# Values' inner products: one matmul of 256 moving columns, written to two places of a PSUM bank, instead of two of 128

## The chip, the cores and the metric

The kernel runs on one core of one Trainium2 chip. The metric is the device time of one execution in microseconds (us). The engines are called PE (TensorE, matmuls), PEld (the weight loads of TensorE, which overlap the matmuls), DVE (VectorE), ACT (ScalarE), POOL (GpSimd) and SP (SyncE, which issues the DMAs). All data are fp32. In the profile every fp32 matmul of the code shows as two MATMUL records, each with its own LDWEIGHTS: the code's 392 matmuls of the gates give 784 records at line 366.

## The reference, cut to what matters

The input x (1024 tokens of 512 features, two batches of 512 tokens) is layer-normalised to xn. Attention makes values and gates from it for 32 heads of 128 dimensions:

```
qkv  = silu(hidden_states @ qkv_w.T)         # q, k, v of every head
gate = sigmoid(hidden_states @ gate_w.T)
...                                          # decaying linear attention over blocks, RMS norm
return gate * normed @ out_w.T
```

A feed-forward part with low-rank experts is added. This case is about `v`, a third of `qkv`: xn times the values' weights, 1024 x 512 times 512 x 4096.

## The kernel before

There are two large stages. The first, the front stage (to about 432 us in the profile), normalises x and computes all values and all gates, which it stores to DRAM. The second computes queries and keys, the attention and the output product. Only the front stage holds the change.

**Sets, rounds, products.** The large products are done by Strassen's scheme in its seven-product form, at two levels. The front stage has eight sets (`n` = 0 to 7); a set is eight heads (two groups of four, `u` = 0 and 1), even sets are values and odd sets are gates. A set has seven outer products, called rounds (`q` = 1 to 7), 56 in all in the list `rounds`; a round has seven inner products (`i` = 1 to 7). An inner product fills one PSUM bank of 128 partitions x 512 fp32, for both groups.

**Which operand moves.** For gates (line 366) the weights `a[:, u]` are stationary and 256 tokens `x_` move: two matmuls, one for each `u`, each with 256 moving columns. For values (line 362) the tokens are stationary, in two pieces of 128 (`j`), and the weights of one group, 128 columns, move: four matmuls of 128 moving columns. The bank is laid out as (u, j, d), so the pieces `j` = 0 of both groups are not neighbours.

**Order.** A round is one turn of a loop over `SLOTS = ((0, 1), (0, 5), (0, 2), (1, 7), (0, 6), (0, 3), (1, 4))`: a pair is (rounds back, inner product). So products 7 and 4 of a round are done within the next one, and where a set of values meets a set of gates, lines 362 and 366 alternate. After each product, `after` says what follows: after product 1, ACT copies the bank `pa` to a new bank (line 427), and product 2, two slots later, adds onto `pa`, so that its first weight load waits for that copy. After product 6 ACT copies again (line 434). The other results are added by DVE (lines 401, 405, 413, 420) or copied by ACT (403, 422); finished ones get Silu or Tanh on ACT (379, 381) and are stored by a DMA on SP (383). The banks are three of tag `fr` and four named `sd` (`seeded`).

**Operands.** `encode` (on POOL, two rounds ahead) makes the weights' sums of a round: four small ones `e` of 128x256 (lines 191 to 194), and for some rounds one or two large ones `s` of 128x1024 (line 177). Products 3, 5, 6 and 7 read `e` (product 3 the last part), products 1, 2 and 4 read the set's weights `raw` or a large sum `s`. `load_set` loads a set's weights from where round `q` = 2 of the set before begins. The order on every engine is that of the code; semaphores come from the tile framework.

Of the kernel before, what the change touches and what calls it, by code (L numbers as in the profile page):

```python
# [40 lines left out]
P = 128  # L41
# [18 lines left out]
def attn_moe_kernel(ctx: ExitStack, tc: tile.TileContext, x, qk_w, v_w, gate_w, out_w, norm_w,  # L60
                    decay, base_w, base_b, router_a_w, lora_b, out):
    nc = tc.nc
# [135 lines left out]
    for n in range(NSET):  # L198
        start = {0: [(0, 1), (1, 1), (0, 6)], 1: [(1, 6), (0, 4)]}.get(n, [(n, 1), (n - 1, 4), (n, 6)])
# [154 lines left out]
    def inner_product(o, r, i, first):  # L354
        n, q = rounds[r]
        a = operand[n, q][i]
        x_ = {1: xo[q][:, 0, :HB], 2: xo[q][:, 1, :HB], 3: xo[q][:, 1, HB:], 4: xt[q - 1][:, 3],
              5: xt[q - 1][:, 0], 6: xt[q - 1][:, 1], 7: xt[q - 1][:, 2]}[i]
        for u in range(2):
            if n % 2 == 0:  # L360
                for j in range(2):
                    nc.tensor.matmul(o[:, (2 * u + j) * P : (2 * u + j + 1) * P], x_[:, j * P : (j + 1) * P],  # L362
                                     a[:, u], start=first and u == 0 and j == 0, stop=True,
                                     skip_group_check=True)
            else:
                nc.tensor.matmul(o[:, u * HB : (u + 1) * HB], a[:, u], x_, start=first and u == 0, stop=True,  # L366
                                 skip_group_check=True)
# [76 lines left out]
    for k in range(7 * len(rounds) + 7):  # L444
        r0, m = divmod(k, 7)
        if m == 0:
            if r0 + 2 < len(rounds):
                encode(*rounds[r0 + 2])
            if r0 < len(rounds):
                n, q = rounds[r0]  # L450
                state_of[r0] = {}
                for _, to in ADDED[q]:
                    if isinstance(to, str):
                        outer_sums[n, to] = aw2.tile([P, 4, 512], F32, tag="sum", name="sum", bufs=4)
                if q == 2 and 0 < n < NSET - 1:
                    load_set(n + 1)
                if (n, q) == (NSET - 1, 2):
                    load_pair(0)
                    for i in range(2):
                        load_unit(i)  # L460
        back, i = SLOTS[m]
        r = r0 - back
        if not 0 <= r < len(rounds):
            continue
        st = state_of[r]
        if i in (1, 5):
            st["pa" if i == 1 else "pc"] = bank("fr")
        inner_product(st[{1: "pa", 2: "pa", 5: "pc", 3: "pc", 6: "pb", 7: "pd", 4: "pd"}[i]], r, i, i in (1, 5))
        after(r, i)
# [182 lines left out]
    for i in range(H * B + 2):  # L652
        p, part = divmod(i, 4)
# [18 lines left out]
        for stage in range(3):  # L672
            j = i - stage
# [141 lines left out]
```

## Time and profile before

| | |
|---|---|
| median of three runs | 1240.96 us (1240.21 to 1243.94) |
| the profiled execution's own time | 1241.71 us |
| its span (first to last instruction) | 1239.9 us |
| PE busy | 1207.4 us, 97% of the span |
| DVE, POOL, ACT busy | 629.1, 592.8, 366.1 us |
| granted PE clock, mean | 0.993 |
| PE busy from 120 to 400 us | 276.7 of 280 us |

A row of the profile's list of groups reads: line, engine, operation, output<-input by the program's tile names, shapes, count, then busy time and mean duration of one, then the engine's idle time before such instructions and what ended it. Durations of neighbouring matmuls overlap, since a matmul's end lies after the next one's start; the pace of PE is therefore read from the starts of consecutive records, in the timeline. There a row gives the start, the length of the merged group, the engine, line, operation, tiles, shape and count.

### The profile page before, as it was taken

The numbers are of one execution on the slowest core, as the hardware profiler recorded it, in microseconds if no ns is written. First come the engines' busy times: TensorE is split into PE (matmuls) and PEld (weight loads), VectorE is DVE, ScalarE is ACT, GpSimd is POOL, SyncE is SP. The second block draws the span as 40 slices with busy tenths as digits, with TensorE's granted clock in tenths as the row PEclk, the third lists the DMA queues.
The fourth block names the chain that finished last, engine by engine and source line by source line (L and its number), as shares of the span: only waits on it lengthen the run. The fifth ranks groups of instructions, "written<-read, shape, count | busy, mean of one in ns | idle before, by whom it ended". The sixth has DMA issues, their size and how long they took to land.

```text
span 1239.9 us, 17100 instructions
## 1 busy us (share of the span) xinstructions
PE 1207.4 (97%) x6328; PEld 914.3 (74%) x6328; DVE 629.1 (51%) x1104; ACT 366.1 (30%) x648; POOL 592.8 (48%) x662
## 2 busy tenths in 40 slices
PE   6789999999999999999999999999999999999998
PEld 4369889899899745666666666666666669888887
DVE  5757666766766624444444434444444444455333
ACT  2124444444444422223222222222232332320000
POOL 3926568758756241434433433433333343655552
PEclk9989999999999999999999999999999999999999
DMA  8012543452442353343443443343334333843221
GB/s 315 0 68 75 173 151 121 153 170 96 161 161 103 123 166 91 119 135 112 145 140 103 125 134 102 117 125 118 116 114 128 120 97 108 309 150 122 93 92 52
DMA packets 102706, 158.17 MB, mean 128 GB/s; under 512 B 8800, under 2 KB 68192, under 8 KB 101344
## 3 DMA queue, kind: packets, MB, share of 16 engines
q1 hardware_dynamic: 102624, 157.09, 38.2%
q8 instruction: 50, 0.82, 0.3%
q14 instruction: 32, 0.26, 0.1%
HBM read 102.53 MB, written 54.53 MB: 127 GB/s over the span
## 4 chain that ended last, share of the span: by engine, by line
PE 93%; DVE 5%; issue 1%; ACT 1%; DMA 0%; SPq 0%; DVEq 0%; ACTq 0%
PE ps_ch L488 31%; PE ps_ch L645 9%; PE ps_at L80 8%; PE ps_sc L80 8%; PE ps_fr L362 7%; PE ps_fr L366 7%; PE sd L362 5%; PE sd L366 5%; PE ps_sc L645 4%; PE ps_at L645 2%; PE sd L80 2%; PE ps_sc L550 2%; DVE z L405 1%; DVE sum L405 1%; PE ps_ra L80 1%
## 5 line engine op out<-in xcount | busy, mean ns | idle before, releaser
L488 PE MATMUL ps_ch<-xsum,ws 128*128 128x512 f32 x384 | 180.0, 593 | 0.0
L562 POOL TENSOR_TENSOR qd<-q,mask 128x384 f32<-128x384 f32 x64 | 64.2, 1003 | 219.9 <-PE ps_at L80 214.8
L488 PE MATMUL ps_ch<-xnT,w 128*128 128x512 f32 x256 | 122.2, 600 | 0.8 <-DVE z L405 0.8
L488 PEld LDWEIGHTS ps_ch<-xsum,ws 128*128 128x128 f32 x384 | 68.5, 191 | 63.2 <-issue 63.2
L80 PEld LDWEIGHTS ps_at<-scores,v 128*128 128x128 f32 x512 | 77.4, 192 | 28.0 <-issue 27.7
L126 POOL TENSOR_TENSOR ws<-w 128x256 f32<-128x256 f32 x32 | 23.4, 730 | 154.3 <-DMA w<-in_qk_w 154.3
L503 DVE TENSOR_TENSOR c<-ps_ch,u 128x512 f32<-128x512 f32 x96 | 66.4, 691 | 58.4 <-PE ps_ch L488 58.4
L588 DVE SCALAR_TENSOR_TENSOR gT<-gate,ps_at 128x512 f32<-128x512 f32 x64 | 44.0, 687 | 97.5 <-ACT sq L585 94.5
L645 PE MATMUL ps_ch<-wsum,gsum 128*128 128x256 f32 x384 | 89.1, 379 | 0.0
L80 PE MATMUL ps_at<-scores,v 128*128 128x128 f32 x512 | 88.4, 275 | 0.0
L585 ACT ACTIVATE sq<-ps_at 128x512 f32<-128x512 f32 x62 | 37.0, 597 | 155.2 <-PE ps_at L80 155.1
L586 POOL TENSOR_TENSOR ssq<-ssq,sq 128x512 f32<-128x512 f32 x62 | 79.2, 1278 | 6.5 <-ACT sq L585 6.5
L645 PEld LDWEIGHTS ps_ch<-wsum,gsum 128*128 128x128 f32 x384 | 72.3, 190 | 9.5
L80 PE MATMUL ps_at<-qd,state 128*128 128x128 f32 x384 | 74.2, 275 | 0.0
L80 PEld LDWEIGHTS ps_sc<-v,kd 128*128 128x128 f32 x384 | 52.8, 191 | 28.4 <-issue 28.2
L633 POOL TENSOR_TENSOR wsum<-wo 128x256 f32<-128x256 f32 x32 | 25.3, 790 | 93.0 <-PE ps_ch L645 37.4
L488 PEld LDWEIGHTS ps_ch<-xnT,w 128*128 128x128 f32 x256 | 44.4, 192 | 34.2 <-issue 33.1
L503 DVE TENSOR_TENSOR u<-ps_ch,p 128x512 f32<-128x512 f32 x32 | 22.1, 692 | 91.4 <-PE ps_ch L488 85.5
L80 PE MATMUL ps_sc<-q,k 128*128 128x128 f32 x512 | 67.6, 275 | 0.0
L552 ACT ACTIVATE kd<-ps_sc,mask 128x384 f32<-128x384 f32 x64 | 37.2, 580 | 89.8 <-PE ps_sc L550 89.8
L626 DVE TENSOR_TENSOR gsum<-gated 128x256 f32<-128x256 f32 x32 | 15.1, 470 | 95.2 <-PE ps_sc L645 66.7
L80 PEld LDWEIGHTS ps_sc<-q,k 128*128 128x128 f32 x512 | 62.2, 192 | 0.0
(224 smaller groups left out, 2633.6 us busy)
## 6 DMA issues: line engine op xcount, KB each, us to landing
w<-in_qk_w SPq DMA_DIRECT2D x32, 512.0 KB, 4.1
v_kept<-z SPq DMA_DIRECT2D x64, 256.0 KB, 2.4
gate_kept<-z SPq DMA_DIRECT2D x64, 256.0 KB, 2.4
v<-v_kept SPq DMA_DIRECT2D x64, 256.0 KB, 2.6
gate<-gate_kept SPq DMA_DIRECT2D x64, 256.0 KB, 3.2
g_kept<-gT SPq DMA_DIRECT2D x64, 256.0 KB, 2.5
gated<-g_kept SPq DMA_DIRECT2D x32, 512.0 KB, 3.7
raw<-in_v_w SPq DMA_DIRECT2D x8, 1024.0 KB, 6.6
```

The costliest lines, as they stand in the source:

```text
L80: nc.tensor.matmul(o, lhsT, rhs, start=start, stop=stop)
L362: nc.tensor.matmul(o[:, (2 * u + j) * P : (2 * u + j + 1) * P], x_[:, j * P : (j + 1) * P], a[:, u], start=first and u == 0 and j == 0, st ...
L366: nc.tensor.matmul(o[:, u * HB : (u + 1) * HB], a[:, u], x_, start=first and u == 0, stop=True, skip_group_check=True)
L488: nc.tensor.matmul(o, a[:, c, :], b[:, c, :], start=first and c == 0, stop=c == 1, skip_group_check=True)
L503: nc.vector.tensor_tensor(o, p, t, ALU.add)
L552: nc.scalar.activation(kd.rearrange("p j d -> p (j d)"), pk[:, : (TB - 1) * P], AF.Copy, scale=mask[:, 0, P - 1 : P])
L562: nc.gpsimd.tensor_tensor(qd, q[:, P:].rearrange("p (j n) -> p j n", j=TB - 1), mask[:, 1, :].unsqueeze(1).to_broadcast([P, TB - 1, P]), A ...
L585: nc.scalar.activation(sq, pa, AF.Square)
L586: nc.gpsimd.tensor_tensor(ssq[b], ssq[b], sq, ALU.add)
L588: nc.vector.scalar_tensor_tensor(gT, gate.pop((head, b)), 1.0, pa, ALU.add, ALU.mult)
L633: nc.gpsimd.tensor_tensor(t[:, 0], b12, b11, ALU.subtract)
L645: nc.tensor.matmul(sums[n][:, i * HO : (i + 1) * HO], l[:, i * P : (i + 1) * P], r, start=p == 0 and i == 0, stop=p == NP - 1, skip_group_ ...
```

## The change

For values, the inner loop over `j` is gone. For each piece `u` of 128 tokens one matmul is issued; its moving operand is `a` whole, 128 columns of the first group and 128 of the second, and its output is two runs of 128 columns, 256 columns apart in the bank. (`u` in the new lines counts the pieces of tokens, and `g` the groups.) The values written and their places are the same.

```
         for u in range(2):
             if n % 2 == 0:
-                for j in range(2):
-                    nc.tensor.matmul(o[:, (2 * u + j) * P : (2 * u + j + 1) * P], x_[:, j * P : (j + 1) * P],
-                                     a[:, u], start=first and u == 0 and j == 0, stop=True,
-                                     skip_group_check=True)
+
+                nc.tensor.matmul(o.rearrange("p (g j d) -> p j g d", g=2, j=2)[:, u], x_[:, u * P : (u + 1) * P],
+                                 a, start=first and u == 0, stop=True, skip_group_check=True)
             else:
                 nc.tensor.matmul(o[:, u * HB : (u + 1) * HB], a[:, u], x_, start=first and u == 0, stop=True,
                                  skip_group_check=True)
```

An inner product of the values thus has 2 matmuls (4 records) in place of 4 (8 records). There are 4 even sets x 7 rounds x 7 products = 196 of them. The moving operand of products 3, 5, 6 and 7 is one run of 256 elements; of products 1, 2 and 4 it is two runs of 128, 512 elements apart in a sum `s` and 2048 apart in `raw`.

## The prediction

> **What bounds the kernel now.** I read the page's busy times first, then the chain that ended last, then, for the front stage alone, the timeline of PE and the waits. The busy times and the chain:
>
> ```profile
> PE 1207.4 (97%) x6328; PEld 914.3 (74%) x6328; DVE 629.1 (51%) x1104; ACT 366.1 (30%) x648; POOL 592.8 (48%) x662
> ...
> PE 93%; DVE 5%; issue 1%; ACT 1%; DMA 0%; SPq 0%; DVEq 0%; ACTq 0%
> PE ps_ch L488 31%; PE ps_ch L645 9%; PE ps_at L80 8%; PE ps_sc L80 8%; PE ps_fr L362 7%; PE ps_fr L366 7%; PE sd L362 5%; PE sd L366 5%; PE ps_sc L645 4%; PE ps_at L645 2%; PE sd L80 2%; PE ps_sc L550 2%; DVE z L405 1%; DVE sum L405 1%; PE ps_ra L80 1%
> ```
>
> PE is the bound and line 362 is 12% of the chain (7% and 5%), so time taken from it is on the path. How much a record costs is its distance to the next start, not its duration of 275 ns. The timeline of PE shows one undisturbed round of values (q = 7 of set 6), and one of gates (q = 7 of set 7):
>
> ```profile
> 367.10 1.06 PE L362 MATMUL ps_fr<-s,xsum 128*128 128x128 f32 x8
> 367.99 1.06 PE L362 MATMUL ps_fr<-e,xt 128*128 128x128 f32 x8
> 368.88 1.09 PE L362 MATMUL ps_fr<-s,xsum 128*128 128x128 f32 x8
> 369.81 1.95 PE L362 MATMUL sd<-e,xt 128*128 128x128 f32 x16
> 371.60 1.06 PE L362 MATMUL ps_fr<-e,xsum 128*128 128x128 f32 x8
> 372.49 1.06 PE L362 MATMUL sd<-s,xt 128*128 128x128 f32 x8
> 373.38 0.39 PE L362 MATMUL ps_fr<-s,xnT 128*128 128x128 f32 x2
> ```
>
> ```profile
> 410.74 1.03 PE L366 MATMUL ps_fr<-xsum,s 128*128 128x256 f32 x4
> 411.60 1.03 PE L366 MATMUL ps_fr<-xt,e 128*128 128x256 f32 x4
> 412.47 1.09 PE L366 MATMUL ps_fr<-xsum,s 128*128 128x256 f32 x4
> 413.39 1.89 PE L366 MATMUL sd<-xt,e 128*128 128x256 f32 x8
> 415.12 1.03 PE L366 MATMUL ps_fr<-xsum,e 128*128 128x256 f32 x4
> 415.98 1.03 PE L366 MATMUL sd<-xt,s 128*128 128x256 f32 x4
> 416.85 0.38 PE L366 MATMUL ps_fr<-xnT,s 128*128 128x256 f32 x1
> ```
>
> The reader should see that eight records of 128 columns take 0.89 us (367.10 to 367.99) and four of 256 take 0.86 (410.74 to 411.60). From the records to the nanosecond: 893 and 863 ns, that is 111.6 and 215.8 ns each. The third product of both rounds takes longer, 0.93 us: it is product 2, which waits for the copy of line 427. Whole rounds: 373.38 - 367.10 = 6.28 us against 416.85 - 410.74 = 6.11. The gates do the same amount of arithmetic in the shape that the values are to get.
>
> The waits tell of the copy:
>
> ```profile
> PEld ps_fr L366 <- ACT sd L427: 7.7, 27, 0.8
> ...
> PEld ps_fr L362 <- ACT sd L427: 2.3, 2, 2.0
> ```
>
> In nearly every gates' round the weight load of product 2 comes late; in values' rounds it is late too, but by less (0.04 us at 368.81, under what the list shows).
>
> **What the Trainium skill says.** "TensorE: Matmul & The Clock Gate", in "Wait — 56ns, not 53.3ns?", gives a fixed 2.5 ns per matmul on top of columns / 2.4 GHz. The trace agrees if an fp32 record is two cycles a column: 256 x 2 / 2.4 + 2.5 = 215.8 ns (215.8 measured) and 512: 429.2 (429 at line 488). For 128 it gives 109.2, which the transposes of line 550 have (109); line 362 has 111.6, 2.4 more. "Back-to-back issue gap" on that page says that weight load and matmul together set the spacing; the weight loads' shortest distance here is about 108 ns (412.425 to 412.533), so at 128 columns they are nearly the bound, and at 256 they are covered twice over. "PSUM — Partial Sum Buffer", "Specifications (TRN2)", says that any non-contiguous access slows matmuls significantly; "Advanced Engine Details and Errata", "PSUM Cachelines", narrows that to every two consecutive elements being contiguous. No matmul in this trace has more than one run in its moving operand, and the code has none before with two runs in its output, so neither can be checked yet. "SBUF — State Buffer", "SBUF: two separate sides", says that a DVE instruction with two SBUF inputs and a POOL one lock each other out; the trace agrees (below).
>
> **The change part by part.**
>
> 1. Records removed and lengthened: 196 products x (8 x 111.6 - 4 x 215.8 = 893 - 863 = 30 ns) = 5.9 us less on PE. This takes 215.8 ns for a record of two runs from line 366's one run; its bounds are in the rivals. The 784 weight loads that go (192 ns each) lie beside matmuls; their only cost on the path is the 2.4 ns per record counted here.
> 2. Given back at product 2, in each of the 28 values' rounds. The copy starts when product 1 is out and takes 0.57 us, and product 5, which covers it, becomes 30 ns shorter. In the rounds shown, products 5 and 2 take 894 + 927 ns with values and 864 + 927 with gates: the wait grows from 34 to 64 ns, 28 x 30 = 0.8 us. All later products queue behind that weight load; DVE and ACT get product 2 no later than in a gates' round.
> 3. More in rounds q = 5 and q = 6, where an ACT activation stands ahead of the copy. q = 5: a values' round lasts 367.10 - 360.78 = 6.32 us, a gates' 410.74 - 404.51 = 6.23, so that 0.09 is gained there and not 0.17: 4 x 0.08 = 0.3 us. q = 6: products 5 and 2 take 962 + 995 ns with values and 992 + 967 with gates, 30 ns more given back in three rounds, 0.1 us.
> 4. Semaphores, DMAs, POOL's, DVE's and ACT's instructions: the same number in the same order. The cover of POOL's sums shrinks with the rounds, by 0.17 us each. POOL waited 40.9 + 37.5 us for PE between 100 and 430 us, so it is ahead; without that lead, as around 150 to 165 us, where it is busy without a break, up to three values' rounds would pass their 0.5 us on as a wait.
> 5. What is late next: DVE where POOL locks it out. Where sets meet, a sum of two SBUF tiles meets a large sum on POOL:
>
> ```profile
> 155.88 2.80 POOL L177 TENSOR_TENSOR s<-raw 128x1024 f32<-128x1024 f32 x1
> ...
> 156.39 2.83 DVE L405 TENSOR_TENSOR z<-c,sum 128x512 f32<-128x512 f32 x1
> ...
> 159.80 0.58 ACT L427 COPY sd<-ps_fr 128x512 f32<-128x512 f32 x1
> ...
> 160.43 0.82 PE L362 MATMUL ps_fr<-raw,xnT 128*128 128x128 f32 x5 [1.82 <-ACT sd L427]
> ```
>
> The DVE sum takes 2.83 us for 0.68, the next activation waits for DVE, the copy stands behind it, and PE stands 2 us. Adding up how far products exceed the usual time at the six such crossings from 100 to 345 us gives about 0.9, 2.4, 0.4, 0.1, 0.6 and 1.4 us, 5.8 in all. Whether the two meet depends on tenths of a microsecond; the change shifts PE and DVE by that much against POOL, which follows the weights' DMAs there. I take no change on average. With some 0.8 us of spread per crossing, six of them spread by about 2 us to either side.
>
> Sum: 5.9 - 0.8 - 0.3 - 0.1 = 4.7 us, and 0.2 I take off for point 4: 4.5 us. The profiled execution took 1241.7 us (span 1239.9); it would take 1237.2. The median of the runs lies 0.75 below the profiled one: **1236.5 us**. The second stage is fed by PE alone at its start and moves forward whole: PE is busy for all of 500 to 1000 us.
>
> **The rivals.** A difference of 0.3%, 3.7 us, is about what a measurement of this kernel can tell from no change.
>
> *Gain eaten by the crossings, or by a record that is not as cheap as line 366's.* If collisions cost 3 us more than now, 1.5 us remain: about 1239.5. Much the same comes out if a two-run record costs 5 ns more than a one-run record (784 x 5 = 3.9 of the 5.9 us; most of point 2 then goes too): 1239. For it: one meeting cost 2 us in the trace, and point 4. Against it: crossings of both kinds are met now, and they may as well get better.
>
> *Slower, by the two runs.* If PE stops between the runs of an output, each of the 784 records pays. The point from which it decides is 5.9 us / 784 = 7.5 ns for equal time (what points 2 and 3 give back is then not taken either), and 7.5 + 3.7 / 784 = 12.2 ns for slower by 0.3%. As a price I take the 25 ns below which, by the TensorE page ("Wait — 56ns, not 53.3ns?"), no two matmuls start apart, as an estimate of a restart: 784 x 25 = 19.6 us, less 5.9: 1254.7. The sentence in the PSUM page speaks for it. Against it, the runs are 512 bytes long and even, so the narrower rule is met, as it is in the moving operand. The unknown is bounded below by the one-run record (no gain is in sight beyond: its 215.8 ns are the streaming time plus 2.5), and above by half speed, 784 x 216 = 169 us, which I hold for nearly excluded.
>
> *The change does nothing.* If a run costs what a matmul of its own did (111.6 ns), the time stays at 1241.
>
> **How the numbers follow.** The forecast (4.5 us give or take the crossings' 2) has 0.84: of it, about two thirds lie beyond 3.7 us. The eaten or void gain has 0.08, the slower rival 0.08. Hence faster 0.57, same 0.34 (0.27 from the forecast's lower part, 0.07 of the eaten gain), slower 0.09. The range reaches from a gain of 7.5 us to the eaten gain's far side: 1233.5 to 1241.5; left out are most of the slower rival and the tails.
>
> **What would show it right or wrong.** Right: in the timeline, the values' products as four records, 0.86 us from start to start, undisturbed rounds of 6.11 us, product 2 at 0.93 us with the weight load's wait for the copy now listed for values as for gates. Products 1 and 2, which read two runs, should pace like 5 and 6, which read one; if only 1 and 2 are slower, it is the read; if all are, it is the write. Wrong: a pace above 220 ns; the six crossings adding up to 8 us or more; or a stop on POOL's `e`. A start of the second stage (432 us now) not 4 to 5 us earlier would say that the front stage gave the gain back.

## The result, and the profile after

The changed kernel takes 1238.41 us (median of 22 runs, 1235.25 to 1241.49) against 1240.74 us before (22 runs, 1237.82 to 1244.18): the ratio is 0.9981 with a 95% interval from 0.9972 to 0.9990. A second series gave 0.9988 (0.9979 to 0.9997; 22 runs against 27). The change is a gain of 2.4 us by the first ratio and 1.5 us by the second, where 4.5 were forecast. The time lies in the range, which is 8 us wide; the gain is about half of the forecast, or less.

The profiled execution took 1238.33 us. The page's busy times and its chain, as for the kernel before (the lines after the change have numbers one lower):

```profile
PE 1200.8 (97%) x5544; PEld 882.8 (71%) x5544; DVE 628.3 (51%) x1104; ACT 366.4 (30%) x648; POOL 591.5 (48%) x662
...
PE 92%; DVE 6%; issue 1%; ACT 1%; DMA 0%; SPq 0%; DVEq 0%; ACTq 0%
PE ps_ch L487 31%; PE ps_ch L644 9%; PE ps_at L80 8%; PE ps_sc L80 8%; PE ps_fr L365 7%; PE ps_fr L362 7%; PE sd L365 5%; PE sd L362 5%; PE ps_sc L644 4%; PE ps_at L644 2%; PE sd L80 2%; PE ps_sc L549 2%; DVE z L404 2%; DVE sum L404 1%; PE ps_ra L80 1%
```

The 784 records are gone (6328 to 5544), and PE's busy time is 6.6 us less. DVE has 6% of the chain where it had 5%; a second profile of the kernel before has 6% too, so that this alone says little. The same undisturbed round as in the prediction (q = 7 of set 6), in the timeline of PE after:

```profile
364.25 1.03 PE L362 MATMUL ps_fr<-s,xsum 128*128 128x256 f32 x4
365.11 1.03 PE L362 MATMUL ps_fr<-e,xt 128*128 128x256 f32 x4
365.98 1.09 PE L362 MATMUL ps_fr<-s,xsum 128*128 128x256 f32 x4
366.90 1.89 PE L362 MATMUL sd<-e,xt 128*128 128x256 f32 x8
368.63 1.03 PE L362 MATMUL ps_fr<-e,xsum 128*128 128x256 f32 x4
369.49 1.03 PE L362 MATMUL sd<-s,xt 128*128 128x256 f32 x4
370.36 0.81 PE L362 MATMUL ps_fr<-s,xnT 128*128 128x256 f32 x3
```

A product is four records and takes 0.86 us, the round 370.36 - 364.25 = 6.11 us, as the gates' rounds do. The records' starts give 216 ns for a record whose moving operand is two runs (products 1 and 2, line `ps_fr<-s,xsum`) and for one whose operand is one run (products 5, 3); the output is two runs in both. The rounds do what was forecast. What else happens is seen where set 6 meets set 7, on all engines:

```profile
374.68 2.36 POOL L177 TENSOR_TENSOR s<-raw 128x1024 f32<-128x1024 f32 x1
...
375.16 2.43 DVE L404 TENSOR_TENSOR sum<-c,sum 128x512 f32<-128x512 f32 x1
...
377.51 1.21 DVE L404 TENSOR_TENSOR z<-c,sum 128x512 f32<-128x512 f32 x1
...
379.92 0.92 PE L365 MATMUL ps_fr<-xnT,raw 128*128 128x256 f32 x3 [1.57 <-ACT sd L426]
```

The large sum on POOL starts at 374.68, and the DVE sum of two SBUF tiles, at 375.16, lasts until POOL's has ended; PE stops 1.6 us behind it. In the profile before, the same DVE sum fell near that large sum's end and took 0.95 us, and PE did not stop there:

```profile
375.65 2.82 POOL L177 TENSOR_TENSOR s<-raw 128x1024 f32<-128x1024 f32 x1
...
378.07 0.95 DVE L405 TENSOR_TENSOR sum<-c,sum 128x512 f32<-128x512 f32 x1
```

This pair does not make the stop a mark of the change: in a second profile of the kernel before (taken with the last experiment) PE stops here too, for 1.4 us.

To place the rest I split each profiled execution by starts of records on PE: the setup (to the first product of the third round), the front stage (from there to product 4 of the last round), and the second stage (from its first to its last record). In us:

| | setup | front stage | second stage |
|---|---|---|---|
| before | 87.04 | 344.28 | 802.62 |
| after | 86.15 | 343.48 | 800.92 |

So of the 3.4 us between these two executions 0.8 came from the front stage, 0.9 from the setup and 1.7 from the second stage. The change lies in what is here called the front stage, but for one round of values in the setup, and should have brought 4.5 there. The setup took 85.1 to 87.0 us over all profiles of this case, so that it adds 1 us or so to the difference between any two executions.

### The profile page after: what moved, and what is told of

Same layout as the page of the kernel before. It is cut to its first block, busy times and chain, and to the rows that moved or that the text cites. A ratio compares the mean times of both kernels' runs of the same rounds, so it can differ in the third digit from the quotient of the medians.

```text
span 1236.5 us, 15529 instructions
## 1 busy us (share of the span) xinstructions
PE 1200.8 (97%) x5544; PEld 882.8 (71%) x5544; DVE 628.3 (51%) x1104; ACT 366.4 (30%) x648; POOL 591.5 (48%) x662
## 4 chain that ended last, share of the span: by engine, by line
PE 92%; DVE 6%; issue 1%; ACT 1%; DMA 0%; SPq 0%; DVEq 0%; ACTq 0%
PE ps_ch L487 31%; PE ps_ch L644 9%; PE ps_at L80 8%; PE ps_sc L80 8%; PE ps_fr L365 7%; PE ps_fr L362 7%; PE sd L365 5%; PE sd L362 5%; PE ps_sc L644 4%; PE ps_at L644 2%; PE sd L80 2%; PE ps_sc L549 2%; DVE z L404 2%; DVE sum L404 1%; PE ps_ra L80 1%
```

## The experiments

### The crossings taken out of both forms

Theory 1: what is missing was taken at the crossings. The edit keeps `c`, the intermediate sum of round q = 7, in PSUM, so that no DVE addition after it has two SBUF inputs. It computes the same.

```
         def summed(v, more):
...
-            c = temp("c")
+            c = v if i == 3 else bank("ra")
             nc.vector.tensor_tensor(c, v, more, ALU.add)
```

> The old form, with the intermediate sum c of round q = 7 kept in PSUM (in product 3 in its own bank, in product 7 in the bank that only the setup uses), so that no sum of two SBUF tiles is left on DVE in the front stage. Theory 1 (the crossings, where such a sum and a large sum on POOL lock each other out, took about half of the gain): the stops of 0.1 to 2.4 us where sets meet go, no addition of line 405 lasts over 0.8 us, and the time falls by 4 to 6 us, to about 1235.5. Theory 2 (the stops come from the weights' DMAs or POOL's sums being late, whatever DVE does): the stops stay and the time is within 1 us of before.

> The new form with the same move of c to PSUM. Theory 1: with the crossings out of both kernels the whole of the change's worth shows: 4.7 us (4 to 5.4) less than the old form with c in PSUM, about 1231, some 9.5 us under before. Rival (the new form loses its other half outside the crossings, in the records, at the copies or in the second stage): the distance to the old form with c in PSUM stays at 2.3 us.

Measured: the old form takes 1232.44 us (0.9935 of before, 0.9922 to 0.9948), the new one 1230.01 (0.9908, 0.9892 to 0.9924). The old form falls by 8.5 us, more than the 4 to 6 of theory 1. By the profiles its front stage falls by 5.9 us, and the new form's by 9.6 (the table below against the one above); the rest lies in the setup and in the second stage, to which the edit does nothing. So the crossings cost 6 us or more, and they cost it in both forms. The distance between the forms stayed at 2.4 us, as the rival had it. The trace of the new form shows that the lock is gone; DVE and POOL at the crossing from set 6 to set 7:

```profile
366.67 0.69 DVE L404 TENSOR_TENSOR sum<-ps_ra,sum 128x512 f32<-128x512 f32 x1
367.28 0.68 DVE L404 TENSOR_TENSOR z<-ps_ra,sum 128x512 f32<-128x512 f32 x1
```

```profile
365.46 2.37 POOL L177 TENSOR_TENSOR s<-raw 128x1024 f32<-128x1024 f32 x1
```

The additions with a PSUM input take 0.69 us each beside the large sum. The stages of the two traces:

| | setup | front stage | second stage |
|---|---|---|---|
| old form, c in PSUM | 85.61 | 338.35 | 800.92 |
| new form, c in PSUM | 85.80 | 333.91 | 802.62 |

With the crossings out, the front stage is 4.44 us shorter. The 1.7 us that the second stage took longer have one place. Of the new form, PE's timeline at the end of the front stage, and the busy times in windows of 3.41 us (the columns after each engine's busy time are counts; PEclk is the granted clock):

```profile
417.47 1.03 PE L365 MATMUL sd<-xt,e 128*128 128x256 f32 x4
419.72 1.13 PE L365 MATMUL sd<-xt,raw 128*128 128x256 f32 x4 [1.23 <-DVE z L400]
421.63 3.66 PE L487 MATMUL ps_ch<-xnT,w 128*128 128x512 f32 x4 [0.78 <-DVE z L404]
425.09 1.09 PE L487 MATMUL ps_ch<-xsum,ws 128*128 128x512 f32 x2
```

```profile
418.39:421.80 3.41, 1.40 (x6) 0.85 (x6) 1.97 (x4) 1.99 (x4) 0.00 (x0) 1.00 0.40 137
421.80:425.21 3.41, 3.41 (x5) 1.35 (x6) 0.00 (x0) 0.49 (x1) 0.00 (x0) 0.50 1.02 299
425.21:428.62 3.41, 3.41 (x10) 1.50 (x9) 0.69 (x1) 0.59 (x1) 2.60 (x4) 1.00 0.81 269
```

PE waits twice for the last round's additions. The window in which it was busy for 1.40 us of 3.41 is followed by one with half the clock, in which four matmuls of 512 columns take 425.09 - 421.63 = 3.46 us. In the old form, whose front stage ends elsewhere in such a window, the same four are twice as fast:

```profile
425.88 1.98 PE L488 MATMUL ps_ch<-xnT,w 128*128 128x512 f32 x4 [0.78 <-DVE z L405]
427.70 2.74 PE L488 MATMUL ps_ch<-xsum,ws 128*128 128x512 f32 x6
```

and its windows there have 2.18 and 2.63 us of PE:

```profile
421.25:424.66 3.41, 2.18 (x10) 1.60 (x9) 2.56 (x4) 1.86 (x3) 0.00 (x0) 1.00 0.41 143
424.66:428.07 3.41, 2.63 (x7) 1.08 (x7) 0.69 (x1) 0.63 (x1) 0.00 (x0) 1.00 1.02 274
```

The times of the new form fall in two groups that go with the mean clock: four executions of 1229.9 to 1230.2 us at 0.993, two of 1227.6 and 1227.7 at 0.996. All six of the old form lie between 1232.0 and 1233.1, at 0.994 or 0.996. One window of half clock takes 0.5 x 3.41 / 1230 = 0.0014 from the mean, so that the two groups are two windows apart: one at the end of the front stage and, it seems, one in the setup, where a half clock of varying length stands in every profile.

### The new form in some sets only

The form was chosen by set: `n != 6` in one kernel, `n == 6` in the other, and the old loop over `j` for the other sets of values.

> The new form in sets 0, 2 and 4, the old form in set 6. In the trace after, the first round of set 7 stops for 1.7 us, and before it does not. If the pace of the set just before a crossing decides whether DVE and POOL meet there, this stop is gone (under 0.3 us) and the other crossings are as after, within 0.4 us each. If each crossing is drawn anew in every execution (by when the weights land), the stops differ at several crossings.

> The new form in set 6 alone. If the pace of the set before decides, the stop of about 1.7 us in the first round of set 7 is there, and the crossings ahead of set 6 are as before (the one from set 5 to set 6 about 1.4 us). If each is drawn anew, this cannot be told beforehand.

Measured, in single executions: 1238.15 and 1240.20 us. I added up by how much products exceed the usual time in rounds q = 7, q = 3 and the next set's q = 1, for the crossings into sets 1 to 7:

| | 1 | 2 | 3 | 4 | 5 | 6 | 7 | sum, us |
|---|---|---|---|---|---|---|---|---|
| before | 0.5 | 2.5 | 0.5 | 0.1 | 0.6 | 1.5 | 0.0 | 5.6 |
| set 6 alone | 0.5 | 2.8 | 1.8 | 1.4 | 0.3 | 0.7 | 0.8 | 8.2 |
| all but set 6 | 0.7 | 3.6 | 1.2 | 0.2 | 0.3 | 1.5 | 1.6 | 9.0 |
| after | 0.7 | 3.2 | 0.6 | 0.1 | 0.8 | 2.0 | 1.8 | 9.3 |

The idea that the pace of the set just before decides falls: with the old form in set 6 the crossing into set 7 still cost 1.6 us (1.3 of it one round earlier than in the trace after, in round q = 3 of set 6), and with the new form there alone it was 0.8. Crossings into sets 3 and 4, far from the edit, changed too. Two executions of the same kernel differ as much: in the two profiles of the kernel before, the crossing into set 4 costs 0.1 and 0.8 us, and the one into set 7 0.0 and 1.6. So the later crossings are largely drawn anew in each execution. The first two are not. In the eight profiles of this case with c in SBUF, four have the old form in sets 0, 2 and 4 and four the new one: into set 1 the old form costs 0.5 us in each and the new one 0.7 in each, and into set 2 it is 2.3 to 2.8 us against 3.2 to 4.6 (in the two highest with a half clock, shown in the last experiment).

### PE kept busy at the end of the front stage

Theory 3: the half clock hides the change's worth in the kernels with c in PSUM. Two matmuls that nothing reads are issued near PE's last gaps (called fillers below); in the trace both run in the first of the two gaps, ahead of product 4.

```
+    def fill():
+        mm(bank("fr"), ident, xnT[0][:, 0, :], True, True)
...
+        if r == len(rounds) - 1 and i == 4:
+            fill()
         inner_product(...)
         after(r, i)
+    fill()
```

> The old form with c in PSUM, and one more matmul of 512 columns, whose result nothing reads, in each of the two gaps where PE waits for the last round's additions at the end of the front stage. Theory 3 (in some executions the granted clock is halved for 3.4 us after those gaps, which costs 1.7 us of the second stage; it happens to fall on the new form more often): the trace of this form had no halved stretch there, so the time stays within 0.5 us of the 1232.4 without the fillers. Theory 4 (the second stage has nothing to do with it): the same.

> The new form with c in PSUM and the same two fillers. Its trace without them shows the halved stretch from 421.8 to 425.2 us. Theory 3: the stretch is gone in every run, the time falls by about 2.2 us to 1227.7 with a spread under 1.5 us, and lies 4.7 us (4.2 to 5.2) under the old form with both. Theory 4: the distance stays at 2.4 us and the time near 1230.

> The kernel before with the two fillers alone. Theory 3: it loses the halved stretch, which its trace has from 433.4 to 436.8 us, in those executions that have it: 0 to 2 us less, about 1239.8. Theory 4: no change.

> The kernel after with the two fillers alone. Theory 3: 4.7 us less than the kernel before with the fillers, give or take 1.5 us for the crossings, which are in both, about 1235. Theory 4: 2.3 us less.

| | time, us | ratio to before (95%) | setup | front stage | second stage |
|---|---|---|---|---|---|
| old form, c in PSUM, fillers | 1233.53 | 0.9940 (0.9927 to 0.9952) | 86.66 | 338.66 | 800.93 |
| new form, c in PSUM, fillers | 1229.08 | 0.9899 (0.9884 to 0.9914) | 86.52 | 334.25 | 800.92 |
| before, fillers | 1241.32 | 1.0002 (0.9993 to 1.0011) | 86.59 | 346.60 | 800.92 |
| after, fillers | 1237.17 | 0.9969 (0.9958 to 0.9979) | 85.16 | 346.00 | 800.92 |

The distance with c in PSUM is now 4.45 us, as theory 3 had it, and 4.41 in the front stages. The second stage takes 800.92 us in all four, and no execution of the pair with c in PSUM has the lower clock. The fillers themselves cost 0.3 us in the front stage. The four times missed their forecasts by 1.1 us (old form, c in PSUM), 1.4, 1.5 and 2.2 us (after), all upward: the first two profiled executions had setups 1.0 and 0.7 us longer than without fillers, and the kernel before did not get faster at all. The distances are what the theory rests on. Without c in PSUM the distance is 4.1 us, but two intervals of about 0.001 each leave some 1.7 us of doubt; the front stages of the two profiled executions are only 0.6 apart, though the profiled one of the new form (1239.75 us) was the slowest of its ten.

### The copy ahead of product 2 covered by two products

Both kernels with c in PSUM and the fillers; products 7 and 2 change places in a round.

```
-    SLOTS = ((0, 1), (0, 5), (0, 2), (1, 7), (0, 6), (0, 3), (1, 4))
+    SLOTS = ((0, 1), (0, 5), (1, 7), (0, 2), (0, 6), (0, 3), (1, 4))
```

> The old form with c in PSUM and the fillers, and products 7 and 2 exchanged in the order of a round, so that the copy of line 427 is covered by two products instead of one. Point 2 and 3 of the prediction (product 2 waits for the copy): its weight load is no longer late; of the waits in this form, 0.033 us in each of 28 values' rounds, 0.064 in each of 28 gates' rounds, and another 0.1 in the rounds q = 5 and 6 of the gates and q = 6 of the values, some 4 us go, to about 1229.5. If those stretches are something else, such as a record's own cost, the time stays at 1233.5.

> The new form with the same three edits. If products 2's waits are what gave 1.2 us of the 5.9 back, the time falls by some 5.5 us to about 1223.5, and the distance to the old form with the same edits grows from 4.4 to 5.9 us, the whole of point 1 (196 products of 30 ns). If not, the distance stays at 4.4.

Measured: 1228.73 us with the old form (0.9899 of before, 0.9882 to 0.9916) and 1222.57 with the new one (0.9849, 0.9834 to 0.9864). They fell by 4.8 and 6.5 us, of which 4.0 and 5.3 in the front stages (now 334.67 and 329.00) and the rest in the setups; the forecasts were some 4 and some 5.5. The distance grew from 4.45 to 6.2 us, 5.7 in the front stages. In the waits of 100 to 415 us, the new form without the exchange (c in PSUM) has

```profile
PEld ps_fr L365 <- ACT sd L426: 6.4, 27, 0.4
PEld ps_fr L362 <- ACT sd L426: 5.6, 24, 0.4
```

and with it one such wait of 0.2 us is left. The last of these kernels is the fastest of the case, 1.5% under the kernel before.

### Both kernels once more

> The kernel after, once more, for the part of the missing gain that the runs with c in PSUM do not explain. If the crossings cost more in the new form on average (some 1.6 us, by the executions with a granted clock of 0.994), its front stage, which takes 333.9 us without them, takes 343 to 345 us, and its runs with a clock of 0.994 lie 2.8 us under those of before. If the crossings cost the same, the front stage takes about 342 and these runs lie 4.4 us under.

> The kernel before, once more, as the other side of the same comparison: its front stage, 338.4 us without the crossings, takes 345 to 347 us.

Measured: 1240.12 us after (median of 22), 1240.78 before (27); the means are 1239.55 and 1240.93. The profiled front stages took 345.57 us (after) and 345.30 (before), and the crossings' sums were 11.3 and 6.7 us. Together with the two pairs above that have c in SBUF everywhere, a front stage exceeds its counterpart with c in PSUM (and the same fillers) by

| | |
|---|---|
| old form | 5.9, 7.0, 7.9 us |
| new form | 9.6, 11.7, 11.8 us |

The new form's crossings are dearer in these three profiles each, by 4 us in the mean. That may be too much: two of the three have a half clock at a crossing (below), and one of them was the slowest of its ten executions. The executions' mean clock says more, as there are more of them: of 68 executions of the kernel before that ran beside these experiments, 52 have a clock of 0.994 and a mean of 1240.5 us, 16 one of 0.993 and 1242.0; of 44 after (both series), 21 have 0.994 and 1237.9, 20 have 0.993 or less and 1240.4 (3 more have 0.995 or 0.996). Like with like the new form is then 2.6 us faster at 0.994 (2.2 in the last series alone, where the forecast was 2.8 for dearer crossings and 4.4 for equal ones), and by the mean clock about half of its executions have one more half-clock window, where it was a quarter before. (A shorter half clock in the setup and one more window later add up to the same mean, so that the groups are rough.)

Two things are seen inside the dearer crossings. One is PE waiting for POOL. The waits of weight loads for the small sums `e`, from 100 to 430 us, first before and then after:

```profile
PEld ps_fr L366 <- POOL e L191: 1.0, 1, 1.0
PEld ps_fr L366 <- POOL e L193: 0.3, 1, 0.3
PEld ps_fr L362 <- POOL e L191: 0.2, 1, 0.2
```

```profile
PEld ps_fr L365 <- POOL e L191: 1.5, 1, 1.5
PEld ps_fr L365 <- POOL e L193: 1.0, 1, 1.0
PEld ps_fr L362 <- POOL e L191: 0.6, 1, 0.6
```

That is 1.5 us before and 3.1 after. In the second profiles it is 1.2 and 3.3 us, with the fillers 2.5 and 3.9, and with c in PSUM there is none. All of these waits are in round q = 3 of a set, just ahead of the next one. The lock holds POOL up as well: some of its sums on lines 191 and 193 take 1.2 us in the traces before and after, where the others take 0.7; with c in PSUM all take 0.7 to 0.8.

The other is the clock. A trace tells where such a window may come from: in the second profile after, at the crossing into set 2, the timeline of DVE, that of PE and the windows are

```profile
155.23 2.84 DVE L404 TENSOR_TENSOR z<-c,sum 128x512 f32<-128x512 f32 x1
```

```profile
156.37 1.03 PE L362 MATMUL ps_fr<-e,xt 128*128 128x256 f32 x4
159.27 1.86 PE L362 MATMUL ps_fr<-raw,xnT 128*128 128x256 f32 x4 [1.88 <-ACT sd L426]
160.93 1.91 PE L365 MATMUL sd<-xt,e 128*128 128x256 f32 x4
162.64 1.18 PE L362 MATMUL sd<-e,xt 128*128 128x256 f32 x4
```

```profile
156.10:159.50 3.40, 1.52 (x7) 1.02 (x7) 3.40 (x4) 1.11 (x2) 3.40 (x4) 1.00 0.13 44
159.50:162.90 3.40, 3.40 (x9) 2.69 (x9) 0.99 (x3) 2.11 (x4) 3.32 (x3) 0.50 0.48 168
```

DVE is locked out for 2 us, PE stops, is busy for 1.52 us of the window, and gets half the clock for the next: products of 0.86 us take 1.7, and a stop of 2 us at a crossing costs more than 3. The profile after with the fillers has the same (half clock from 158.3 to 161.7 us). None of the three old-form profiles with c in SBUF has it at a crossing, but they are not far from it: PE was busy for 1.69, 1.62 and 2.06 us of the window with the same stop. Nor has the first profile after, with 1.69 us.

## Why the prediction was right, and where its size was off

**Point 1, the records: right.** Records of two runs have the pace of one-run records, 216 ns, so that 30 ns a product are saved. With the waits for the copy gone the whole is seen: 6.2 us by the times, 5.7 by the front stages, for 5.9 forecast. The slower rival (a restart of 25 ns between the runs) and the case that the change does nothing are out; so is the sentence of "PSUM — Partial Sum Buffer", "Specifications (TRN2)", that any non-contiguous access slows matmuls significantly, for runs of 128 fp32: the 784 records show nothing of it. "Advanced Engine Details and Errata", "PSUM Cachelines", has that sentence too; its narrower wording, two consecutive elements, is met by these runs, and no run here tests it further.

**Points 2 and 3, given back at product 2: right.** The forecast was 4.7 us net; the front stages with c in PSUM are 4.44 and 4.41 us apart. The copy's wait is now listed for values as for gates (24 and 27 times), and exchanging two products takes it away and brings the distance back to about 5.9.

**Point 4, POOL's lead: mis-sized.** From POOL's own waits for PE I read it as ahead and took off 0.2 us. But the trace before already had weight loads waiting 1.5 us for `e` where sets meet, and after it was 3.1 us, so the stop on `e` that I had named as a sign of being wrong is there. The cover that shrinks, up to 0.5 us for three values' rounds, fits in size the first of these waits, which is 0.2 us in each of the four profiles with the old form there and 0.6 in each of the four with the new one. With c in PSUM no such wait is left, so these waits belong to the crossings.

**Point 5, the crossings: the term that was mis-sized.** I priced them at 5.8 us in both forms, from one execution, and took no change on average. They cost 5.9 to 7.9 us in the old form by the front stages (8.5 by the times, 1240.9 us less 1232.4), and in the new one 4 us more than in the old by three profiles each, or some 2 us by the executions at like clock: 4.4 us of worth without crossings, 2.6 with. Two more of my signs of being wrong came: the six crossings up to 345 us add up to 7.4 us in one profile after and to 9.0 in the other (8 was the mark), and the second stage starts at 431.5 us against 433.2, 1.7 us earlier and not 4 to 5. The gain eaten by the crossings, to which I gave 0.08 with the void change, is near to what happened. The mechanism that I had named, a DVE sum of two SBUF tiles and a large sum on POOL ("SBUF — State Buffer", "SBUF: two separate sides"), is shown: with one input in PSUM the same additions run beside POOL in 0.69 us, and 6 us or more of the front stage go. That the measured time still lies in the range is owed to the range's width: a gain beyond 3.7 us, to which I gave the most, did not come.

**What I had left out is the clock.** The trace before had it, from 433.4 to 436.8 us:

```profile
429.99:433.40 3.41, 1.39 (x6) 0.84 (x6) 1.97 (x4) 1.99 (x4) 0.00 (x0) 1.00 0.40 136
433.40:436.81 3.41, 3.41 (x5) 1.35 (x6) 0.00 (x0) 0.49 (x1) 0.00 (x0) 0.50 0.99 297
```

I took the second stage as moved forward whole; it takes 800.92 or 802.62 us according to where the end of the front stage falls. It was the cause of most of the missing half between the two kernels with c in PSUM (1.7 of some 2 us), shown by the trace and by the fillers. Between the two kernels of the change my estimate is a smaller part: about a quarter more executions with one more such window, of 1.7 us each where it falls into dense matmuls, make some 0.4 us. The fillers speak for more: with them the distance is 4.1 us, though they leave the crossings as they are. Its doubt of 1.7 us reaches to the 2.4 us of the first series, so this does not settle it.

Together the two account for what is missing: with c in PSUM and the fillers the distance is 4.45 us. What stays open is how the missing 2 to 3 us divide between the crossings and the clock, and why the new form's crossings are dearer. A shift of PE and DVE against POOL by tenths of a microsecond is enough, and the later crossings vary between executions of one kernel. For the crossings into sets 1 and 2 the difference is there in all eight profiles. That the shorter rounds cause it by shrinking the cover of POOL's sums is argued, and no run shows it apart from the rest.

## What to carry to other kernels

A matmul wrote two runs of a bank and read two runs of SBUF at full pace here, with runs of 128 fp32, and 128 moving columns of fp32 were worth joining to 256: 30 ns for each eight records. Before such a gain of 0.4% is counted, look for what swallows it: a DVE addition with two SBUF inputs beside long POOL instructions, and gaps of PE of 1 to 2 us, which here could cost 1.7 us more after they had ended, by how they lay in the windows of the clock. Two other edits were worth more than the 2 us that the change gained: 6 to 8 us in the old form by keeping one operand in PSUM, and 4.0 (old form) and 5.3 us (new form) of front stage by giving a copy two products of cover.

## What the runs showed of the hardware

- The granted clock changed in windows of 3.41 us. Windows with 1.39 to 1.52 us of PE were followed by half the clock for the next whole window, though PE was busy again in it; those with 1.62, 1.69, 1.97 or more were not. One with 1.53 us, in the kernel with the new form in all sets but 6, was not either, so that in this measure the border lies near 1.53 us, 45% of the window, and is not sharp: the ends of matmuls are modelled in the profile. "TensorE: Matmul & The Clock Gate", "What's actually happening", has the window and the two clocks; the border is from these traces.
- In both profiles that had such a window at the start of the second stage it cost 1.70 us (802.62 - 800.92 us for 3792 records), and the same gaps at the end of the front stage brought it or not by where they lay in the windows. The setup has a half clock too: one of 13.7 us there was released at 69.1 to 71.6 us (in one of the profiled executions after 10.2 us, at 68.1), and the third round started at 85.2 to 87.0 us (85.05 in that one).
- An addition on DVE with one PSUM and one SBUF input took 0.69 us beside a POOL sum of 2.37 us; with two SBUF inputs it took up to 2.84 (0.68 where the two did not meet).
